# A two-layer stretch of a decoder: sparse self-attention whose keys and values are copied by DMA instead of projected once per offset

## The chip, the core and the metric

The kernel runs on one NeuronCore of a Trainium2 chip. Five engines have their own instruction streams and meet at semaphores: TensorE (PE in the profile; PEld is its weight load), VectorE (DVE), ScalarE (ACT), GpSimd (POOL) and SyncE (SP, which here only issues DMAs). Every stream is executed in the order in which it was written down; an instruction that waits holds up all that stand behind it on its engine. The metric is the device time of one execution in microseconds, lower is better.

## What is computed

A pre-norm decoder of four layers on x of shape (8, 256, 128), float32, each layer with a self-attention, a cross-attention and a feed-forward part. Each part reads the layer norm of x and adds its result to x:

```python
x = x + _L1_ffn_ref(_layernorm(x), W_r, W_k, W_v, mu_r, mu_k)
x = x + _L2_attn_ref(_layernorm(x), W_qkv, b_qkv, W_proj, b_proj)
x = x + _L2_xattn_ref(_layernorm(x), ctx, Wq, bq, Wk, bk, Wv, bv, Wo, bo)
```

The change lies in `L2_attn`: 16 heads of 8 channels, 256 tokens per batch, and a mask under which token i sees only the tokens i - o for o in 0, 1, 2, 4, 8, 16, 32, 64, 128, where they exist. So each token has at most nine keys; the softmax is over nine scores per head. The kernel computes it without a score matrix: for each offset o it needs the keys and values of token i - o beside the query of token i. `L2_xattn`, which follows, is a dense cross-attention of 256 queries on 512 keys per batch, 16 heads.

## The kernel before

**Layout.** x stays in SBUF with tokens on the partitions, two half batches of 128 tokens for each of the 8 batches. `E.xt(b, back)` is the transposed norm of batch b (channels on partitions, tokens along the free dimension), with 128 zero columns ahead of it, so that `back=o` reads the tokens moved down by o.

**`_l2_attn` (L1066).** It works on half batches t = 2b + half. `weigh(t)` projects the query (`fa_qps`, L1084), and then, for each offset, projects keys and values of the moved tokens (`fa_kvps`, L1097): 8 projections for the first half and 9 for the second, each of 256 output columns. VectorE multiplies each key block by the query into `fa_pr` (L1098), ScalarE copies the values to `fa_v` (L1101). Then come the sum over the 8 channels of a head (L1107), the key bias (L1108), the mask, the softmax over the offsets (L1113 to L1118, exp on ScalarE L1115), values times weights on GpSimd (L1120), and the first step of the sum over the offsets, also on GpSimd (L1122). `apply(t)` ends the sum (L1128 to L1132), transposes (`fa_tps`), applies the output projection (`fa_yps`), adds to x, and after the second half takes the norm for the next layer. `through` runs `weigh(t)` and then `apply(t - 1)`, so one half batch's GpSimd work lies beside the next one's projections. Both use two buffers per tile.

**Two places.** Batches 0 and 1 are run by `_middle` (L1215) beside the end of the layers before. The other six batches, and the last three of the four `_l1_ffn` units that come ahead of them, are a *guest*: a Python generator (`rest`, L1220) which `_heads_attention` advances while it writes down the instructions of `L2_xattn`. Each `yield` is a place where the host's own instructions come in between.

**The host.** `_heads_attention` (L463) writes down 128 steps t, 16 heads for each of 8 batches. Step t has the scores for the row maxima (`mh_sps`, two 128x512 tiles, three PSUM banks in all; VectorE reduces each to `mh_nm`, L527), the transposed scores of the step eight earlier with their exponentials (`mh_bsps`, L581), and now and then a product with the values (`mh_ops`). `visit(rate)` (L663) advances the guest by `rate` yields a step: 1.25 here (L697). Ahead of head 9 of batch b, the guest is advanced until batch b + 1 has been normed (L686). Matrix products and transposes of the host and of the guest go through `mm` and `turn_over` (L447), which keep them in the order in which the program wrote them. The other engines' instructions are ordered by a scheduler with its own estimates.

**DMAs.** For each batch, keys and queries of `L2_xattn` are spread over partitions by 12 SBUF to SBUF DMAs on SP's queue (`mh_k`, L422, and `mh_q`, L427). Ahead of the first scores, ScalarE fills those buffers with constants (L368), in memory that is free only when the layers before are done.

Of the kernel before, what the change touches and what calls it, by code (L numbers as in the profile page):

```python
# [40 lines left out]
P = 128  # L41
# [418 lines left out]
            f()  # L460


def _heads_attention(E, ctx, causal=False, mask=None, key_bias=None, gate=False, guest=None, known=(0,)):  # L463

# [190 lines left out]
    def normed(b, z):  # L657
        _normed(E, b, z, pg, turn_over)

    normed_already = set(range(B) if guest is None else known)  # L660
    credit = [0.0]

    def visit(rate):  # L663

        credit[0] += rate
        while credit[0] >= 1:
            credit[0] -= 1
            normed_already.add(next(guest, None))
# [4 lines left out]
    while t < end or todo:  # L673
        now[0] = t
        b, h = divmod(t, H)
        if b + 1 < B:
            if h == 0:
                early, spread, values = hd.steps(b + 1)
            if causal:

                at = {2: early[:1], 3: early[1:2], 4: early[2:], 13: [values]}
                at.update({5 + i: spread[i : i + 1] for i in range(6)})
            else:
                at = {6: early[:1], 8: spread[:1], 9: spread[1:2] + early[1:], 13: spread[5:] + [values]}
                at.update({10 + i: spread[2 + i : 3 + i] for i in range(3)})
            while h == 9 and b + 1 not in normed_already:  # L686
                visit(1)
            for f in at.get(h, ()):
                f()
        if gate and b < B and h == 6:  # L690
            gate_of(b)
        if t < H * B:
            maxima(t)
            if t % 4 == 3:
                turn(t // 4)
        if guest:
            visit(1.25 if 1 in known else 2.4 if t < 9 else 1.4)  # L697
        if t % 4 == 1 and 4 < t < H * B + 2:
            turned(t // 4 - 1)
        if 0 <= t - lag < H * B:  # L700
            exps(t - lag)
        c = t - lag - 4
        if c % 4 == 0 and 0 <= c < H * B:
            combine(c // 4)
        for f in todo.pop(t, ()):
            f()
        if t == H * (B - 2) + 12 + free:
            E.draining()
        t += 1


def _l0(E, names, given_up):

    nc = E.nc
    with ExitStack() as scope, ExitStack() as first:
# [38 lines left out]
                pass  # L754
        for _ in queries:
            pass
        _heads_attention(E, scope, mask=(m, mt), guest=steps)


def _l2_xattn(E, ctx):  # L760
    guest, E.guest = E.guest, None
    _heads_attention(E, ctx, guest=guest, known=(0, 1))


def _l3_attn(E, ctx):
# [254 lines left out]
def _l1_ffn(E, ctx, side="left"):  # L1020
# [6 lines left out]
    def unit(g):  # L1027
        mixed = []
        for i, n in enumerate(("mu_r", "mu_k")):
            t = wk.tile([P, 2, S], F32, name="rk_t")  # L1030
            nc.vector.tensor_scalar(t, E.xt2(g, 1), rest[:, i : i + 1], None, ALU.mult)
            m = wk.tile([P, 2, S], F32, name=f"rk_m{i}")
            nc.vector.scalar_tensor_tensor(m, E.xt2(g), W(n), t, ALU.mult, ALU.add)
            mixed.append(m.rearrange("p b t -> p (b t)"))
        yield
        mr, mk = mixed
        ps = E.banks.rk.tile([P, 512], F32, tag="g", name="rk_kps")
        E.mm(ps, W("wk"), mk, start=True, stop=True)
        k = wk.tile([P, 512], F32, name="rk_k")
        nc.scalar.activation(k, ps, AF.Relu)  # L1040
        nc.scalar.activation(k, k, AF.Square)
        yield
        ps = E.banks.rk.tile([P, 4, D], F32, tag="g", name="rk_rps")
        for t in range(4):
            E.mm(ps[:, t, :], mr[:, t * P : t * P + P], W("wr"), start=True, stop=True)
        r = wk.tile([P, 4, D], F32, name="rk_r")
        nc.scalar.activation(r, ps, AF.Sigmoid)
        yield
        ps = E.banks.rk.tile([P, 4, D], F32, tag="g", name="rk_ops")
# [16 lines left out]
def _l2_attn(E, ctx):  # L1066


    nc, W = E.nc, E.w("L2_attn")
    wk = ctx.enter_context(E.tc.tile_pool(name="fa", bufs=2))  # L1070
    scale = DH ** -0.5
    NO = len(OFFS)
    heads = lambda a: a.rearrange("p (h d) -> p h d", d=DH)
    st = {}

    def weigh(t):
        b, half = divmod(t, 2)
        at = slice(half * P, half * P + P)
        if half == 0:
            E.pre_add(b, W("bo"))  # L1080
        offs = [o for o in OFFS if o < P * (half + 1)]
        no = len(offs)
        ps = E.banks.fa.tile([P, D], F32, tag="g", name="fa_qps")
        E.mm(ps, E.xt(b)[:, at], W("wqkv")[:, :D], start=True, stop=True)  # L1084
        q = wk.tile([P, D], F32, name="fa_q")
        nc.vector.tensor_tensor(q, ps, W("b")[:, :D], ALU.add)

        yield
        qb = wk.tile([P, D], F32, tag="fa_s", name="fa_qb")
        nc.gpsimd.tensor_tensor(qb, q, W("b")[:, D : 2 * D], ALU.mult)  # L1090
        pr = wk.tile([P, NO, D], F32, name="fa_pr")
        v = wk.tile([P, NO, D], F32, name="fa_v")
        for i in range(0, no, 2):
            n = min(2, no - i)
            ps = E.banks.fa.tile([P, 2, 2 * D], F32, tag="g", name="fa_kvps")
            for j in range(n):
                E.mm(ps[:, j, :], E.xt(b, offs[i + j])[:, at], W("wqkv")[:, D:], start=True, stop=True)  # L1097
            nc.vector.tensor_tensor(  # L1098
                pr[:, i : i + n, :], ps[:, :n, :D], q.unsqueeze(1).to_broadcast([P, n, D]), ALU.mult
            )  # L1100
            nc.scalar.copy(v[:, i : i + n, :], ps[:, :n, D:])  # L1101
            yield
        sb = wk.tile([P, H], F32, name="fa_sb")
        nc.vector.tensor_reduce(sb, heads(qb), AX.X, ALU.add)
        sc = wk.tile([P, NO, H], F32, name="fa_sc")
        a = sc[:, :no, :]
        nc.vector.tensor_reduce(a, pr[:, :no, :].rearrange("p o (h d) -> p o h d", d=DH), AX.X, ALU.add)  # L1107
        nc.vector.tensor_tensor(a, a, sb.unsqueeze(1).to_broadcast([P, no, H]), ALU.add)  # L1108
        if half == 0:
            nc.vector.tensor_tensor(a, a, W("fenwick")[:, :no].unsqueeze(2).to_broadcast([P, no, H]), ALU.add)  # L1110
        red = wk.tile([P, H], F32, name="fa_red")
        wide = red.unsqueeze(1).to_broadcast([P, no, H])
        nc.vector.tensor_reduce(red, a.rearrange("p o h -> p h o"), AX.X, ALU.max)  # L1113
        nc.vector.tensor_tensor(a, a, wide, ALU.subtract)
        nc.scalar.activation(a, a, AF.Exp, scale=scale)  # L1115
        nc.vector.tensor_reduce(red, a.rearrange("p o h -> p h o"), AX.X, ALU.add)
        nc.vector.reciprocal(red, red)
        nc.vector.tensor_tensor(a, a, wide, ALU.mult)  # L1118
        v4 = v[:, :no, :].rearrange("p o (h d) -> p o h d", d=DH)
        nc.gpsimd.tensor_tensor(v4, v4, a.unsqueeze(3).to_broadcast([P, no, H, DH]), ALU.mult)  # L1120

        nc.gpsimd.tensor_tensor(v[:, :4, :], v[:, :4, :], v[:, 4:8, :], ALU.add)  # L1122
        st[t] = v, no

    def apply(t):
        v, no = st.pop(t)
        o = wk.tile([P, D], F32, tag="fa_s", name="fa_o")
        nc.vector.tensor_tensor(v[:, :2, :], v[:, :2, :], v[:, 2:4, :], ALU.add)  # L1128
        nc.vector.tensor_tensor(o, v[:, 0, :], W("b")[:, 2 * D :], ALU.add)
        nc.vector.tensor_tensor(o, o, v[:, 1, :], ALU.add)  # L1130
        if no > 8:
            nc.vector.tensor_tensor(o, o, v[:, 8, :], ALU.add)  # L1132
        ps = E.banks.fa.tile([P, P], F32, tag="g", name="fa_tps")
        E.turn_over(ps, o)
        ot = wk.tile([P, P], F32, name="fa_ot")
        nc.scalar.copy(ot, ps)
        yield
        ps = E.banks.fa.tile([P, D], F32, tag="g", name="fa_yps")
        E.mm(ps, ot, W("wo"), start=True, stop=True)
        nc.vector.tensor_tensor(E.x[:, t, :], ps, E.x[:, t, :], ALU.add)  # L1140
        if t % 2:
            z = _norm(E, t // 2)
            yield
            yield
            yield
            _normed(E, t // 2, z, E.banks.ln, E.turn_over)
            yield t // 2

    def through(g, n, ahead=lambda g: ()):

        first, end = 4 * g, 4 * (g + n)
        for t in range(first, end + 1):
            if t < end:
                if t % 4 == 0:
                    yield from ahead(t // 4)
                yield from weigh(t)
            if t > first:
                yield from apply(t - 1)

    return through  # L1160


def _middle(E, names, then):
# [8 lines left out]
    if names != MIDDLE:  # L1172
        for n in names:
            with ExitStack() as scope:
# [4 lines left out]
                    "L2_attn": _l2_attn,  # L1179
                }[n](E, scope, *([pg] if n in MIDDLE[:3] else []))  # L1180
                if n == "L2_attn":
                    _run(unit(0, 4))
                    continue
                for g in range(4):
                    _run(unit(g) or ())
# [26 lines left out]
    begun = E.beginning(then)  # L1212
    if guest:
        next(begun)
    _run(fa(0, 1))  # L1215
    if guest:
        next(begun, None)
    psum.close()
# [1 line left out]
    def rest():  # L1220
# [4 lines left out]
        with ExitStack() as own:  # L1225
            if not guest:
                g = banks(own, "mid_pg2", 6)
                E.banks = SimpleNamespace(fa=g, rk=g, ln=g)
            yield from fa(1, 3, _l1_ffn(E, own))
        last.close()  # L1230
        E.close_weights()

# [434 lines left out]
```

## Time and profile before

| | us |
|---|---|
| runs | 1818.8, 1821.27, 1822.99 (median 1821.27) |
| profiled execution | 1820.01 |
| its span, first to last instruction | 1818.2 |
| `fa` instructions of `_l2_attn`, first and last start | 782.2 to about 1211 |
| first scores of `L2_xattn` | 912.8 |
| last row maxima of `L2_xattn` | 1278.0 |
| TensorE busy over the span | 1483.6 (82%) |
| VectorE busy | 1147.1 (63%) |
| ScalarE busy | 874.4 (48%) |
| GpSimd busy | 515.3 (28%) |

The profile gives, for each stretch of time, how long each engine had an instruction in execution, how many instructions there were, the clock that TensorE was granted (1.00 is full speed), the mean busy share of the 16 DMA engines and the bytes that they moved. For each tile it gives the instructions that write or read it, with the shortest, median and longest duration in ns. For each idle stretch it names the instruction that ended it. "SPq" is the issue of a DMA by SP.

### The profile page before, as it was taken

How to read it: one execution, taken by the hardware profiler on the slowest of the kernel's cores; microseconds unless marked ns; L12 is line 12 of the kernel's file. 1: busy time of each engine (PE TensorE's matmuls, PEld its weight loads, DVE VectorE, ACT ScalarE, POOL GpSimd, SP SyncE). 2: the span in 40 equal slices, each digit the busy share in tenths (PEclk: the TensorE clock that was granted, in tenths of full speed). 3: DMA queues.
4: the chain of work that ended last, by engine and by line, in shares of the span. 5: the costliest groups of instructions: out<-in, count | busy, mean ns of one | idle time of the engine just before them, and what ended most of it. 6: DMA issues, size and time to landing. Idle time of an engine off the chain costs nothing. (4 is left out here: it accounts for less than half of the span.)

```text
span 1818.2 us, 29293 instructions
## 1 busy us (share of the span) xinstructions
PE 1483.6 (82%) x10099; PEld 1070.8 (59%) x10137; DVE 1147.1 (63%) x3869; ACT 874.4 (48%) x1791; POOL 515.3 (28%) x1002
## 2 busy tenths in 40 slices
PE   5689999999989989787378888879635999799976
PEld 3456677766655556455256665656314777677753
DVE  3567666675636676777377777767584665455546
ACT  7245455555642445222645556557412566466621
POOL 3122222222101121333323433331225333344321
PEclk8799999999999999887689999989755999899977
DMA  4011101114000000000111111011002221111000
GB/s 150 12 36 35 26 14 37 35 32 154 12 1 1 1 1 1 0 1 1 26 43 35 36 32 32 14 36 37 17 23 82 66 54 49 47 51 49 26 1 23
DMA packets 47235, 60.42 MB, mean 33 GB/s; under 512 B 5232, under 2 KB 36976, under 8 KB 46448
## 3 DMA queue, kind: packets, MB, share of 16 engines
q1 hardware_dynamic: 44720, 56.99, 11.8%
q8 instruction: 80, 1.31, 0.3%
q10 hardware_dynamic: 2368, 1.57, 0.3%
q14 instruction: 67, 0.55, 0.1%
HBM read 14.50 MB, written 1.05 MB: 9 GB/s over the span
## 5 line engine op out<-in xcount | busy, mean ns | idle before, releaser
L448 PE MATMUL mh_sps<-mh_k,mh_q 96*128 96x512 f32 (+2 forms) x1024 | 321.7, 396 | 46.7 <-DMA mh_q<-mh_qp 16.1
L448 PE MATMUL mh_bsps<-mh_q,mh_k 128*128 128x256 f32 (+1 forms) x1536 | 351.0, 334 | 6.9 <-ACT mh_e L581 4.1
L581 ACT ACTIVATE mh_e<-mh_bsps 128x512 f32<-128x512 f32 x512 | 280.8, 599 | 114.3 <-PE mh_bsps L448 107.1
L448 PEld LDWEIGHTS mh_bsps<-mh_q,mh_k 128*128 128x128 f32 x1536 | 264.6, 197 | 31.8 <-issue 6.7
L448 PEld LDWEIGHTS mh_sps<-mh_k,mh_q 96*128 96x128 f32 x1024 | 171.7, 201 | 94.5 <-issue 37.4
L508 DVE CUSTOM_DVE_ANT_0 mh_rest<-mh_sps,mask_b 128x512 bf16<-128x512 f32 x256 | 167.2, 685 | 84.5 <-PE mh_sps L448 81.3
L448 PE MATMUL mh_ops<-mh_e,mh_v 128*32 128x256 f32 (+1 forms) x3072 | 201.7, 372 | 11.1 <-ACT mh_e L568 10.6
L527 DVE TENSOR_REDUCE mh_nm<-mh_sps 128x1 f32<-128x512 f32 x256 | 164.8, 681 | 32.9 <-PE mh_sps L448 32.5
L448 PEld LDWEIGHTS mh_ops<-mh_e,mh_v 128*32 128x32 f32 x3072 | 96.5, 111 | 81.4 <-ACT mh_e L568 22.1
L568 ACT ACTIVATE mh_e<-mh_bsps 128x384 f32<-128x384 f32 x256 | 116.5, 494 | 49.4 <-PE mh_bsps L448 29.6
L197 POOL TENSOR_SCALAR ln_rstd<-ln_mv 128x2 f32<-128x2 f32 x96 | 22.7, 237 | 392.9 <-DVE ln_mv L195 392.9
L508 DVE CUSTOM_DVE_ANT_0 mh_rest<-mh_sps,km_q 128x128 bf16<-128x128 f32 (+1 forms) x256 | 80.0, 350 | 66.1 <-PE mh_sps L448 63.6
L508 DVE CUSTOM_DVE_ANT_0 mh_rest<-mh_sps,causal 128x128 bf16<-128x128 f32 (+1 forms) x256 | 79.6, 353 | 63.4 <-PE mh_sps L448 46.3
L534 POOL CAST mh_hi<-mh_nm 128x8 fp32r<-128x8 f32 x128 | 25.1, 196 | 332.4 <-DVE mh_nm L508 203.8
L215 ACT COPY xt<-ln_ps 128x256 f32<-128x256 f32 x96 | 36.0, 375 | 160.7 <-PE ln_ps L214 81.6
L546 ACT CAST mh_m<-mh_mps 8x256 fp32r<-8x256 f32 x128 | 46.3, 362 | 97.6 <-PE mh_mps L451 95.7
L611 ACT COPY mh_osb<-mh_ops 128x256 f32<-128x256 f32 x128 | 47.7, 372 | 85.8 <-PE mh_ops L448 85.5
L869 ACT ACTIVATE moe_si<-moe_gps 128x512 f32<-128x512 f32 x64 | 38.0, 597 | 102.1 <-PE moe_gps L867 81.4
L448 PE MATMUL mh_bsps<-mask_t,ident 128*128 128x512 bf16 x219 | 85.0, 388 | 0.4 <-ACT mh_e L581 0.4
L867 PE MATMUL moe_ups<-xt,w_L_ffn 128*128 128x512 f32 x128 | 68.9, 621 | 7.0 <-ACT moe_si L869 4.8
L878 PEld LDWEIGHTS moe_dps<-w_L_ffn,moe_act 128*128 128x128 f32 x512 | 64.6, 200 | 15.9 <-issue 7.5
L201 DVE TENSOR_SCALAR ln_z<-x,ln_mv,ln_rstd 128x128 f32<-128x128 f32 x128 | 42.7, 374 | 48.5 <-POOL ln_rstd L198 48.4
(357 smaller groups left out, 3118.6 us busy)
## 6 DMA issues: line engine op xcount, KB each, us to landing
mh_k<-mh_kp SPq DMA_DIRECT2D x64, 256.0 KB
mh_q<-mh_qp SPq DMA_DIRECT2D x256, 64.0 KB
mh_k<-mh_kp SPq DMA_DIRECT2D x64, 128.0 KB
w_L_ffn<-in_w_L_ffn SPq DMA_DIRECT2D x2, 1558.0 KB
w_L_attn<-in_w_L_attn SPq DMA_DIRECT2D x2, 1056.0 KB
ctx_t<-in_ctx_t SPq DMA_DIRECT2D x4, 512.0 KB
mh_q<-mh_m ACTq DMA_DIRECT2D x128, 8.0 KB
w_L_ffn<-in_w_L_ffn SPq DMA_DIRECT2D x2, 687.0 KB
```

The costliest lines, as they stand in the source:

```text
L201: (engine or nc.vector).tensor_scalar(z[:, q, :], E.x[:, 2 * b + q, :], mv[:, q, 0:1], rstd[:, q : q + 1], ALU.subtract, ALU.mult)
L215: E.nc.scalar.copy(E.xt(b), ps.rearrange("p q t -> p (q t)"))
L448: return self.E.tc.keep_in_program_order(self.E.nc.tensor.matmul(*a, **kw))
L508: nc.vector.tensor_tensor_reduce(rest[:, : scores.shape[1]], scores, lowered, -1.0, -FLOOR, ALU.add, ALU.min, accum_out=at)
L527: nc.vector.tensor_reduce(u.nm[:, c, col], ps, AX.X, ALU.max, negate=True)
L546: nc.scalar.copy(m, ps[:8].rearrange("p c q -> p (c q)"))
L568: nc.scalar.activation(e, ps, AF.Exp, scale=scale)
L581: nc.scalar.activation(e, ps, AF.Exp, scale=scale)
L611: nc.scalar.copy(osbs[b][:, u4 % 2, :], ops)
L867: nc.tensor.matmul(ps, W("w13")[:, o : o + P], xt, start=True, stop=True)
L869: nc.scalar.activation(si, pgate, AF.Silu)
L878: nc.tensor.matmul(ps[:, t, :], act[:, c, t * P : t * P + P], W("w2")[:, o : o + P], start=c == 0, stop=c == 1)
```

## The change

Keys and values of a batch are projected once, without an offset, with the query in the same matrix product (384 columns, `fa_ps`). VectorE adds the bias and writes them to slot 0 of one tile `fa_kv` of [128, 2 halves, 9 offsets, 256], of which there is a single buffer. For the other offsets, 15 DMAs on SP's queue copy slot 0 down by o partitions: rows o to 127 of both halves from rows 0 to 127 - o, and the first o rows of the second half from the last o rows of the first. For the lowest offset the first of these has 127 partitions, then 126, 124, 120, 112, 96 and 64. The rows of the first half that no token reaches are zeroed once, on ScalarE. Products of key and query, and of value and weight, are written over `fa_kv`, and both halves of a batch go through one softmax. `one_batch(b)` has 13 yields and is not overlapped with the next batch; the generator's loop runs over batches.

`_middle` runs only batch 0 instead of batches 0 and 1; batch 1 becomes the guest's first work. The pace of the guest in `L2_xattn` becomes 1.6 yields a step for the first nine steps and 1.2 after. In `_l1_ffn` two tiles share the buffers of two others. What `L0_xattn` does is the same, written with a function for its pace.

```diff
...
-def _heads_attention(E, ctx, causal=False, mask=None, key_bias=None, gate=False, guest=None, known=(0,)):
+def _heads_attention(E, ctx, causal=False, mask=None, key_bias=None, gate=False, guest=None, pace=None):
...
-    normed_already = set(range(B) if guest is None else known)
+    normed_already = set(range(B) if guest is None else (0,))
...
-            visit(1.25 if 1 in known else 2.4 if t < 9 else 1.4)
+            visit(pace(t))
...
-        _heads_attention(E, scope, mask=(m, mt), guest=steps)
+        _heads_attention(E, scope, mask=(m, mt), guest=steps, pace=lambda t: 2.4 if t < 9 else 1.4)
 def _l2_xattn(E, ctx):
     guest, E.guest = E.guest, None
-    _heads_attention(E, ctx, guest=guest, known=(0, 1))
+    _heads_attention(E, ctx, guest=guest, pace=lambda t: 1.6 if t < 9 else 1.2)
...
-            m = wk.tile([P, 2, S], F32, name=f"rk_m{i}")
+            m = wk.tile([P, 2, S], F32, tag=f"rk_m{i}", name=f"rk_m{i}")
-        k = wk.tile([P, 512], F32, name="rk_k")
+        k = wk.tile([P, 512], F32, tag="rk_m1", name="rk_k")
-        r = wk.tile([P, 4, D], F32, name="rk_r")
+        r = wk.tile([P, 4, D], F32, tag="rk_m0", name="rk_r")
...
     nc, W = E.nc, E.w("L2_attn")
+    one = ctx.enter_context(E.tc.tile_pool(name="fa1", bufs=1))
     wk = ctx.enter_context(E.tc.tile_pool(name="fa", bufs=2))
     scale = DH ** -0.5
     NO = len(OFFS)
...
+    kv = one.tile([P, 2, NO, 2 * D], F32, name="fa_kv")
+
+    nc.scalar.copy(
+        kv[:, 0, 1:, :].rearrange("p o c -> p (o c)"), E.plain[:, 0:1].to_broadcast([P, (NO - 1) * 2 * D])
+    )
+    heads = lambda a: a.rearrange("p s o (h d) -> p (s o) h d", d=DH)
+
+    def one_batch(b):
+        E.pre_add(b, W("bo"))
+        q = wk.tile([P, 2, D], F32, name="fa_q")
+        for s in range(2):
+            ps = E.banks.fa.tile([P, 3 * D], F32, tag="g", name="fa_ps")
+            E.mm(ps, E.xt(b)[:, s * P : s * P + P], W("wqkv"), start=True, stop=True)
+            nc.vector.tensor_tensor(kv[:, s, 0, :], ps[:, D:], W("b")[:, D:], ALU.add)
+            nc.vector.tensor_tensor(q[:, s, :], ps[:, :D], W("b")[:, :D], ALU.add)
+        yield
+        for i, o in enumerate(OFFS):
+            if 0 < o < P:
+                nc.sync.dma_start(kv[o:, :, i, :], kv[: P - o, :, 0, :])
+                nc.sync.dma_start(kv[:o, 1, i, :], kv[P - o :, 0, 0, :])
+            elif o:
+                nc.sync.dma_start(kv[:, 1, i, :], kv[:, 0, 0, :])
+        yield
+        yield
+        k, v = kv[:, :, :, :D], kv[:, :, :, D:]
+        nc.vector.tensor_tensor(k, k, q.unsqueeze(2).to_broadcast([P, 2, NO, D]), ALU.mult)
+        yield
+        sc = wk.tile([P, 2, NO, H], F32, name="fa_sc")
+        nc.vector.tensor_reduce(sc.rearrange("p s o h -> p (s o) h"), heads(k), AX.X, ALU.add)
+        nc.vector.tensor_tensor(
+            sc[:, 0, :, :], sc[:, 0, :, :], W("fenwick").unsqueeze(2).to_broadcast([P, NO, H]), ALU.add
+        )
+        red = wk.tile([P, 2, H], F32, name="fa_red")
+        wide = red.unsqueeze(2).to_broadcast([P, 2, NO, H])
+        by_head = sc.rearrange("p s o h -> p s h o")
+        nc.vector.tensor_reduce(red, by_head, AX.X, ALU.max)
+        nc.vector.tensor_tensor(sc, sc, wide, ALU.subtract)
+        nc.scalar.activation(sc, sc, AF.Exp, scale=scale)
+        yield
+        nc.vector.tensor_reduce(red, by_head, AX.X, ALU.add)
         nc.vector.reciprocal(red, red)
...
+        nc.vector.tensor_tensor(sc, sc, wide, ALU.mult)
+        for s in range(2):
+            v4 = v[:, s, :, :].rearrange("p o (h d) -> p o h d", d=DH)
+            nc.gpsimd.tensor_tensor(v4, v4, sc[:, s, :, :].unsqueeze(3).to_broadcast([P, NO, H, DH]), ALU.mult)
+
+        for s in range(2):
+            nc.gpsimd.tensor_tensor(v[:, s, :4, :], v[:, s, :4, :], v[:, s, 4:8, :], ALU.add)
+        yield
+        yield
+        o = wk.tile([P, 2, D], F32, name="fa_o")
+        nc.vector.tensor_tensor(v[:, :, :2, :], v[:, :, :2, :], v[:, :, 2:4, :], ALU.add)
+        nc.vector.tensor_tensor(o, v[:, :, 0, :], v[:, :, 1, :], ALU.add)
+        nc.vector.tensor_tensor(o, o, v[:, :, 8, :], ALU.add)
+        yield
+        ps = E.banks.fa.tile([P, 2, P], F32, tag="g", name="fa_tps")
+        for s in range(2):
+            E.turn_over(ps[:, s, :], o[:, s, :])
+        ot = wk.tile([P, 2, P], F32, name="fa_ot")
         nc.scalar.copy(ot, ps)
         yield
...
+        ps = E.banks.fa.tile([P, 2, D], F32, tag="g", name="fa_yps")
+        for s in range(2):
+            E.mm(ps[:, s, :], ot[:, s, :], W("wo"), start=True, stop=True)
+        E.add(b, ps)
+        z = _norm(E, b)
+        yield
+        yield
+        yield
+        _normed(E, b, z, E.banks.ln, E.turn_over)
+        yield b
+
+    def through(first, end, ahead=lambda g: ()):
+
+        for b in range(first, end):
+            if b % 2 == 0:
+                yield from ahead(b // 2)
+            yield from one_batch(b)
     return through
...
-                    _run(unit(0, 4))
+                    _run(unit(0, 8))
...
-    _run(fa(0, 1))
+    _run(fa(0, 1 if guest else 2))
...
-            yield from fa(1, 3, _l1_ffn(E, own))
+            yield from fa(1 if guest else 2, B, _l1_ffn(E, own))
```

More of the change, by code (lines that the diff above doesn't have):

```diff
@@ L1072, in _l2_attn @@
     NO = len(OFFS)
[L1073 to L1086, printed above, removed]
-        yield
[L1089 to L1116, printed above, removed]
-        nc.vector.reciprocal(red, red)
[L1118 to L1135, printed above, removed]
+    kv = one.tile([P, 2, NO, 2 * D], F32, name="fa_kv")
@@ L1136, in apply @@
         nc.scalar.copy(ot, ps)
         yield
[L1138 to L1158, printed above, removed]
+        ps = E.banks.fa.tile([P, 2, D], F32, tag="g", name="fa_yps")
```

## The prediction

> **What bounds the kernel now.** I read the windows of busy time first, split at the two places where `_l2_attn` runs: 782 to 912 us (beside the layers before), 912 to 1211 (guest in `L2_xattn`), and 1220 to 1280 (the host alone). Columns: busy us and count for PE, PEld, DVE, ACT, POOL, then granted clock, DMA share, GB/s.
>
> ```profile
> 782.00:863.00 81.00, 61.10 (x234) 42.44 (x235) 61.32 (x162) 23.30 (x56) 28.75 (x29) 0.75 0.00 1
> 863.00:912.00 49.00, 17.11 (x58) 11.25 (x56) 17.63 (x51) 28.65 (x27) 14.58 (x18) 0.67 0.13 30
> 912.00:1211.00 299.00, 248.08 (x1739) 180.69 (x1740) 219.62 (x547) 155.87 (x345) 106.06 (x180) 0.93 0.14 34
> 1220.00:1280.00 60.00, 56.85 (x486) 40.42 (x480) 43.65 (x88) 42.90 (x89) 12.33 (x36) 1.00 0.12 29
> ```
>
> The host alone is bound by PE (57 of 60 us). Between 863 and 912 nothing is full: that is a chain of waits. The same windows for the row maxima (L527, DVE) count steps, two to a step:
>
> ```profile
> 912.00:1211.00 299.00, 121.69 (x188) 0.93 0.14 34
> 1220.00:1280.00 60.00, 39.73 (x64) 1.00 0.12 29
> ```
>
> So the host alone takes 60/32 = 1.88 us a step, and with the guest 299/94 = 3.18. Of the 299 us, 94 x 1.88 = 176 are the host's, and about 72 of the 248 busy us are the guest's. By the rows of the tiles, and 8 projections starting in 1.89 us on the timeline:
>
> ```profile
> L448 PE MATMUL fa_kvps<-w_L_attn,xt x204: 377/379/634, 932.0 to 1192.7; 128*128 128x256 f32 x102
> PE fa_tps L451 <- DVE fa_o L1132: 8.8, 1, 8.8
> ```
>
> 204 x 0.24 = 48 us are key and value projections. The rest of the 299, 51 us, is PE idle; lines of the waits that name `fa` tiles (such as the second above) make 21 of it. The guest's own chain hardly stalls PE today: a half batch's work has the next one's projections beside it.
>
> How the stage begins, and what the operations of the chain take (timeline, then tiles; ns are shortest, median, longest):
>
> ```profile
> 862.99 3.60 ACT L368 CAST mh_k<-plain 64x4096 fp32r<-64x4096 f32 x1 [2.35 <-DVE x L1014]
> 912.80 2.35 PE L448 MATMUL mh_sps<-mh_k,mh_q 96*128 96x512 f32 x4 [7.57 <-DMA mh_q<-mh_qp]
> L1107 DVE TENSOR_REDUCE fa_sc<-fa_pr x16: 1161/1278/1353, 822.9 to 1194.0; 128x128 f32<-128x1024 f32 x8, 128x144 f32<-128x1152 f32 x8
> L1120 POOL TENSOR_TENSOR fa_v<-fa_v,fa_sc x16: 1965/2092/2196, 843.4 to 1199.0; 128x1024 f32<-128x1024 f32 x8, 128x1152 f32<-128x1152 f32 x8
> L1122 POOL TENSOR_TENSOR fa_v<-fa_v x16: 1261/1272/1287, 845.5 to 1201.3; 128x512 f32<-128x512 f32 x16
> L427 SPq DMA_DIRECT2D mh_q<-mh_qp x8: 613/613/649, 906.2 to 911.0; - x8
> ```
>
> SP needs 0.613 us for each DMA, and the last of these was usable 912.8 - 911.0 = 1.8 us after its issue began.
>
> **Part 1, the start of the stage: a gain.** Only batch 0 stands ahead of `L2_xattn`. In the changed order ScalarE does, from the first fill on, three fills (3.6 each), one of 0.76, the key bias 0.68, the value copy 0.58, the norm's copy 0.37, another fill 3.6 and the query bias 0.47: 17.3 us. Before, query bias to first scores took 912.8 - 905.7 = 7.1. If the fills start at 863 as now, scores begin at 887. PE loses some 50 projections (12 us) between 782 and 863, where it is busy 61 of 81 us; I take 3 us of it, bounds 0 and 8 (the layers before have their own chains). Start 884, 28.5 us earlier. Batch 0's DMAs are issued near 784 and needed after some 35 us of older VectorE work: free. The zero fill (2048 columns, half a 4096 fill: 1.8 us of ACT, once) lies where ACT is busy 23 of 81 us: free; uncovered, 1.8. Shared tags in `_l1_ffn`: each tile's last reader precedes the new writer anyway; free (1 us a group at worst).
>
> **Part 2, PE, ACT and DVE work of the guest: a gain.** Projections become 7 batches x 2 halves x 2 passes of 384 columns; eight such passes (L918) took 2.75 us, so 0.344 x 28 = 9.6. Transposes and output 6, norms and the three `_l1_ffn` units 15: 31 in place of 72. DVE falls by some 3 us a batch (nine products of 0.41 become one of about 2.6; one softmax for two), ACT by nine copies of 0.37. These two are not the bound here and get nothing. Idle of other causes stays: 51 - 21 = 30, of which I keep 25 as the start is smoother. Stage: 176 + 31 + 25 = 232 us, 67 less than 299. Parts 1 and 2 together: 95 us to the good, before any new wait.
>
> **Part 3, the chain of one batch: a loss.** The batches no longer overlap each other, and PE's order is fixed: between `fa_ps` and `fa_tps` the changed order has the scores of 7, 6, 7, 7, 7 and 6 steps (5 for batch 1), mean 6.6 x 1.88 = 12.4 us of PE work. Then PE stands until the chain is through, with all host steps behind it. VectorE's order is worse: from the key product (L1099) to the last sum (L1127) stands one row maximum at most, so it waits for ScalarE and GpSimd with the maxima behind it. From the end of the DMAs the chain is: product and reduction over 2304 elements, 2.6 each (twice L1107's 1.3); mask, max, subtract, exp, sum, reciprocal, multiply about 3.1; GpSimd 2 x 2.19 + 2 x 1.27 = 6.9; three sums 1.6; handovers 0.3: 17.1. Projection and bias ahead: 2. With D from first issue to last landing, PE's stall is S = 2 + D + 17.1 - 12.4 = D + 6.7; for batch 1, where five steps of scores alone take 6.5 us, D + 12.6. Sum over 7 batches: 7D + 53.
>
> **D, which no row shows.** A batch has 15 DMAs, 1.8 MB in rows of 1 KB. Low end: issue sets the pace, 15 x 0.613 + 1.8 = 11. That needs all 16 engines. The rows here that move much use outer dimensions of 8, 16 or 128. The Trainium skill, page "DMA: Bandwidth & Descriptors", section "Why a DMA increments its semaphore by 16 and not by 1", says that a copy goes to the largest number of engines up to 16 that divides its slowest dimension, starting with the lowest, and gives 127 partitions as the case of one engine. No copy before has such a shape, so the trace neither confirms nor denies it. By that rule 127, 126, 124 and 120 partitions use 1, 14, 4 and 15 engines, and engine 0 gets 254 + 18 + 62 + 16 + 34 (the larger others) + 8 + 11 (small ones) = 403 rows. Time per row:
>
> ```profile
> 904.00:914.00 10.00, 2.43 (x7) 1.34 (x6) 0.39 (x1) 0.85 (x2) 1.78 (x3) 0.50 0.20 52
> 10.00:20.00 10.00, 3.59 (x4) 1.34 (x5) 2.58 (x4) 9.94 (x7) 2.32 (x4) 1.00 0.87 339
> ```
>
> The first window holds 512 rows of 1 KB (`mh_q`) in 0.20 x 160 = 32 engine us: 62 ns. The second, long loads, 339/(16 x 0.87) = 24.4 GB/s an engine: 42 ns. I take 50, since one long queue lies between the two: 403 x 0.05 + 0.6 + 1.8 = 22.6 us. With 42 ns 19.3, with 62 ns 27.6. By the issue row alone the loss is 7 x 11 + 53 = 130; by the page's rule 7 x 22.6 + 53 = 211. I take the rule[...]; its other end stays in the range. `mh_k` and `mh_q` spreads now stand behind these DMAs on SP and on engine 0; they would land some 6 us after D, inside the 17 us chain that PE waits for, so they add nothing; were the chain short, they would be late next. A stalled PE also restarts slowly (clock 0.50 in the window 904 to 914): 0 to 2 us a batch, in the range only, because VectorE sets the pace of the first steps.
>
> **Sum.** -95 + 211 = +116 on the profiled 1820.0: 1936. That execution is 1.3 us under the median of 1821.3, so no correction is made. A difference of 0.2% (3.6 us) is about what the measurement can tell.
>
> **Rivals.**
> A (forecast, 0.72): few engines carry the copies; 1913 at 42 ns, 1936, 1971 at 62 ns (1985 with a slow restart).
> B (0.17): the copies do spread over 16 engines; -95 + 130 = +35: 1855. For it: the 12 spreads per batch of today use 8 or 16 engines. Against: the divisibility of 127.
> C (0.08), faster: the chain is hidden, so that only the PE relief is left. The place is PE's wait at `fa_tps`; the price is S, and it decides at 95/7 = 13.6 us. With row maxima slipping in and steps slower than 1.88 us (the present 3.18 x 6.6 = 21 us would cover all but S = 8 with D = 11), 7 x 8 = 56: 1781. Against: the written order of VectorE, and that steps get slow only by stalling.
> Same (0.03): B with S near 13.6.
>
> **How the numbers follow.** 1936 is A at 50 ns. The range 1850 to 1990 takes in B and A with its slow restart and leaves out C, and A with still slower rows. Faster 0.08, same 0.03, slower 0.89.
>
> **What would show it.** Scores of `L2_xattn` beginning near 884 (part 1). Some 31 us of guest work on PE up to the last `fa_yps` (part 2). PE waits naming `fa_tps` of 25 to 35 us for each of seven batches, and VectorE's key product waiting for DMA `fa_kv` 10 us or more; one DMA engine far busier than the mean share. Waits of about 18 us at `fa_tps` and none of VectorE on DMA would be B. Wrong altogether: no wait at `fa_tps`, or an end of the guest earlier than 1211 us.

## The result, and the profile after

The changed kernel takes 1954.01 us (median of four runs, 1953.41 to 1954.51), against 1822.13 for the kernel before, run beside it: ratio 1.0727, interval 1.0708 to 1.0745. The profiled execution has a span of 1951.6 us, 133.4 more than before, where the prediction had 116 more.

The windows, with the same columns as before: the layers before; the fills ahead of `L2_xattn`; guest and host together; most of the host alone.

```profile
782.00:863.00 81.00, 45.52 (x192) 27.63 (x192) 58.16 (x140) 22.12 (x46) 29.31 (x27) 0.81 0.08 23
863.00:887.00 24.00, 4.54 (x19) 2.47 (x19) 1.63 (x6) 23.86 (x12) 5.49 (x10) 0.66 0.27 66
887.00:1325.00 438.00, 212.53 (x1434) 145.95 (x1438) 220.03 (x437) 135.98 (x271) 108.03 (x172) 0.71 0.19 50
1325.00:1400.00 75.00, 70.89 (x608) 50.05 (x604) 53.08 (x114) 51.91 (x106) 14.26 (x42) 0.96 0.16 37
```

The guest's stage has grown from 299 to 438 us although PE has less to do in it (213 us busy for 248). PE stands idle for 225 us of the stage, and its granted clock is 0.71 in place of 0.93. No other engine is full either: VectorE is busy for half the time. A stage in which everybody is half idle is a chain of waits. Two of the lines of waits (waiting engine and line, releaser, us in all, times, longest) show its links, VectorE for the copies and PE for VectorE's last sum:

```profile
PE fa_tps L451 <- DVE fa_o L1127: 154.4, 7, 32.9
DVE fa_kv L1099 <- DMA fa_kv<-fa_kv: 77.6, 7, 14.7
```

The first guest batch in the timeline (start, us, engine, instruction; in brackets the idle time before it and what ended it):

```profile
886.95 1.19 PE L448 MATMUL mh_sps<-mh_k,mh_q 96*128 96x512 f32 x2 [9.76 <-DMA mh_q<-mh_qp]
...
889.91 1.95 SPq L1093 DMA_DIRECT2D fa_kv<-fa_kv  x3
...
891.96 11.52 SPq L1092 DMA_DIRECT2D fa_kv<-fa_kv  x4
...
909.89 0.60 SPq L1095 DMA_DIRECT2D fa_kv<-fa_kv  x1
...
912.00 2.56 DVE L1099 TENSOR_TENSOR fa_kv<-fa_kv,fa_q 128x2304 f32<-128x2304 f32 x1 [14.67 <-DMA fa_kv<-fa_kv]
...
920.75 4.33 POOL L1118 TENSOR_TENSOR fa_kv<-fa_kv,fa_sc 128x1152 f32<-128x1152 f32 x2 [25.14 <-DVE fa_sc L1115]
...
927.55 0.69 DVE L1125 TENSOR_TENSOR fa_kv<-fa_kv 128x512 f32<-128x512 f32 x1 [6.88 <-POOL fa_kv L1121]
...
929.31 0.66 PE L451 MATMUL fa_tps<-ident,fa_o 128*128 128x128 f32 x2 [32.92 <-DVE fa_o L1127]
```

Read it downwards: scores begin at 886.95, the copies are issued from 889.91 on, the key product starts 22.1 us after the first issue (this is D), the chain behind it takes 17.3 us, and PE has by then waited 32.9 us at the transpose. The four issues in the second SP line took 11.52 us, where four of 0.65 would be 2.6: SP was held for some 9 us. What the DMA engines did meanwhile (window 889 to 914 in 40 slices of 0.625 us; the first line is the mean busy share of the 16 engines in tenths, the second what they moved):

```profile
DMA  0000000000000000001744324676768464450000
GB/s 0 0 0 2 3 7 0 11 13 13 18 25 23 25 25 25 23 25 41 213 157 95 48 80 84 151 195 177 220 210 261 154 159 120 128 203 21 0 0 0
```

For some 5 us the whole core moves 25 GB/s, and then up to 261. The prediction took 24.4 GB/s for one engine at long loads, so this plateau reads as one engine at work, and fifteen that wait for SP to issue; the runs with one more copy test it.

### The profile page after: what moved, and what is told of

Read it like the earlier page. It is cut to its first block, busy times and chain, and to the rows that moved or that the text cites. A ratio compares the mean times of both kernels' runs of the same rounds, so it can differ in the third digit from the quotient of the medians.

```text
span 1951.6 us, 28659 instructions
## 1 busy us (share of the span) xinstructions
PE 1441.3 (74%) x9865; PEld 1025.5 (53%) x9865; DVE 1139.9 (58%) x3701; ACT 854.6 (44%) x1704; POOL 507.4 (26%) x986
## 5 line engine op out<-in xcount | busy, mean ns | idle before, releaser
L448 PE MATMUL mh_sps<-mh_k,mh_q 96*128 96x512 f32 (+2 forms) x1024 | 325.9, 401 | 71.0 <-DMA mh_q<-mh_qp 20.7
L581 ACT ACTIVATE mh_e<-mh_bsps 128x512 f32<-128x512 f32 x512 | 276.6, 599 | 123.5 <-PE mh_bsps L448 96.0
L448 PEld LDWEIGHTS mh_bsps<-mh_q,mh_k 128*128 128x128 f32 x1536 | 268.6, 200 | 55.1 <-ACT mh_e L581 20.5
L448 PE MATMUL mh_ops<-mh_e,mh_v 128*32 128x256 f32 (+1 forms) x3072 | 209.7, 385 | 11.0 <-ACT mh_e L568 10.9
L448 PEld LDWEIGHTS mh_ops<-mh_e,mh_v 128*32 128x32 f32 x3072 | 99.1, 114 | 86.4 <-ACT mh_e L568 22.1
L451 PE MATMUL fa_tps<-ident,fa_o 128*128 128x128 f32 x14 | 4.8, 444 | 154.4 <-DVE fa_o L1127 154.4
L534 POOL CAST mh_hi<-mh_nm 128x8 fp32r<-128x8 f32 x128 | 24.7, 193 | 356.8 <-DVE mh_nm L508 204.6
L448 PE MATMUL mh_bsps<-mask_t,ident 128*128 128x512 bf16 x256 | 99.3, 388 | 0.4 <-ACT mh_e L581 0.4
```

Of the source, the lines that this page charges most:

```text
L448: return self.E.tc.keep_in_program_order(self.E.nc.tensor.matmul(*a, **kw))
L534: nc.gpsimd.tensor_copy(hi, nm)
L581: nc.scalar.activation(e, ps, AF.Exp, scale=scale)
```

## The experiments

### Cutting the odd copies

```diff
-                nc.sync.dma_start(kv[o:, :, i, :], kv[: P - o, :, 0, :])
+                m = (P - o) // 16 * 16
+                nc.sync.dma_start(kv[o : o + m, :, i, :], kv[:m, :, 0, :])
+                if o + m < P:
+                    nc.sync.dma_start(kv[o + m :, :, i, :], kv[m : P - o, :, 0, :])
```

> Each copy of o to 127 is cut in two: the largest multiple of 16 partitions first (112, 112, 112, 112, 112, 96, 64), and the remaining 15, 14, 12 and 8 in a copy of their own: 19 DMAs a batch in place of 15, the same bytes. Theory A (few engines carry the copies): first issue to key product falls from 22 to 26 us to about 14 (19 x 0.613 + 1.8), the key product's waits on DMA from 77.6 us to 20 at most, and the time by 7 x 10 = 70 us to about 1884. Rival, SP's issue sets D: four more issues make each batch 2.5 us longer, about 1970. Rival, the chain behind the copies is all of the loss: within 10 us of 1954.

Measured: 1909.06 us, ratio to before 1.0473 (1.045 to 1.0497): 45 us back, not 70. D (first issue to key product) fell in the seven batches from 22.1, 22.2, 25.7, 25.6, 23.0, 23.1, 23.7 (mean 23.6) to 15.6, 15.9, 23.2, 23.2, 15.8, 15.4, 15.6 (mean 17.8). So the direction of the forecast holds, and its size does not: 19 issues at 0.65 us and 2.1 to the landing make 14.5, and five of the seven batches are within 1.5 us of that. The other two kept a D above 23. SP's own waits name why:

```profile
SPq L1095 <- DMA mh_q<-mh_m: 13.4, 2, 6.8
```

Twice a copy waits some 7 us for a small DMA of the host's, issued by ScalarE. The changed kernel has the same wait in the same two batches (9.6 us in the two together). The copies share no data with that DMA, but they share a semaphore (the counter that tells when a DMA is done): by the trace the DMAs of the stage take eight of them in turn, 24 to 26 DMAs each in the changed kernel, and each of these waits is for the DMA that used the copy's own semaphore last.

### No copies

```diff
-        for i, o in enumerate(OFFS):
-            if 0 < o < P:
-                nc.sync.dma_start(kv[o:, :, i, :], kv[: P - o, :, 0, :])
-                nc.sync.dma_start(kv[:o, 1, i, :], kv[P - o :, 0, 0, :])
-            elif o:
-                nc.sync.dma_start(kv[:, 1, i, :], kv[:, 0, 0, :])
```

> The copies by offset are left out (slots 1 to 8 of both halves are zeroed once and hold what the kernel leaves there), so that only slot 0 is right; every other instruction stays. Theory A says that D was about 23 of a stall of about 30 us, but that the rest of the chain (17 us behind 13 row maxima) is not hidden either: S = 17 for six batches, 13 for the first, stage 232 + 115 = 347 us in place of 434, about 1867. Rival, the copies are all of the loss: about 1727, no PE wait at fa_tps. Rival, the copies cost nothing: 1954.

Measured: 1825.28 us, ratio 1.0013 (1.0002 to 1.0023), 42 us below the forecast and near neither rival. Leaving the copies out takes 129 us away. But without them nothing is gained over before either, so the rest of the new order eats the whole gain of parts 1 and 2. The stage, which begins at 878.7 here, and PE's waits, of this kernel:

```profile
879.00:1200.00 321.00, 208.66 (x1434) 144.26 (x1437) 217.64 (x435) 135.76 (x270) 110.75 (x172) 0.80 0.12 27
```

```profile
PE fa_tps L451 <- DVE fa_o L1122: 62.6, 6, 12.3
PE mh_sps L448 <- DVE mh_nm L527: 28.9, 14, 15.4
```

PE idles 112 us of this stage, 63 of it at the transposes and 29 for row maxima that stand behind the guest's chain in VectorE's order.

The omission takes away more than the copies of the stage. Batch 0's copies are gone too, and its transpose comes at 847.0 us instead of 855.4, so 8 of the 129 us lie ahead of the stage. And VectorE's instructions come out in another order: in five of the seven batches 12 to 14 row maxima stand inside the chain, which then takes 23.2 to 24.7 us, where the changed kernel has four at most. So the 129 us are the copies with that order, which no run separates.

### The early start by itself, in the kernel before

```diff
-            visit(1.25 if 1 in known else 2.4 if t < 9 else 1.4)
+            visit((2.0 if t < 9 else 1.3) if early else 2.4 if t < 9 else 1.4)
...
-    _run(fa(0, 1))
+    _run(fa(0, 1 if guest else 2))
```

(`fa` counts groups of two half batches here in the old line and batches in the new one; `through` runs `2 * g` to `2 * n`.)

> The kernel before, with one part of the change: only batch 0 runs ahead of the cross-attention, batch 1 is the guest's first work, pace 2.0 yields a step for nine steps and 1.3 after. Projections per offset stay. Part 1 of the prediction gives 26 us at the start; batch 1 costs the guest 16 us of PE and about 5 of waits: about 1816. Rival, the early start gains nothing because batch 1 has no cover in the first nine steps (15 us more of waits): 1825 to 1830. Rival, the start is worth the full 26: 1795.

Measured: 1827.59 us, ratio 1.0029 (1.0017 to 1.0041): the rival held, not the 1816 forecast. Row maxima start 23 us earlier (890.2 instead of 913.6) and end 9 us later (1286.9 instead of 1278.0). The batch that no longer delays the start comes back as guest work in a stage where PE is busy for four fifths of the time. An early start, with the pace that goes with it, is worth nothing here.

### One more copy of 127 partitions, and one of 112

```diff
+    spare = one.tile([P, 2, 2 * D], F32, name="fa_spare")
...
+        nc.sync.dma_start(spare[:127, :, :], kv[:127, :, 0, :])
         for i, o in enumerate(OFFS):
```

> Ahead of the copies of each batch stands one more, of 127 partitions to a spare tile that nobody reads (254 rows of 1 KB). Theory A, with 127 partitions on one engine: D grows by 254 rows at 45 to 50 ns, 11 to 13 us, 7 batches 80 to 89 us: about 2038. Rival, the copies spread over 16 engines and the issue sets D: 0.6 to 1 us a batch, about 1960.

> The changed kernel with one more copy ahead of each batch's copies, of 112 partitions instead of the 127 of the run before, into the same spare tile (its data are not used). Theory A (one engine carries a copy of 127 partitions): 16 engines take these 224 rows, so a batch pays one issue on SP, 0.6 us, and at most 0.6 us of transfer: 1958 to 1963 us, key products waiting some 1 us longer a batch. If it is the bytes and not the number of engines, this copy costs nearly what 127 partitions cost (8.4 us a batch): 2005 to 2013.

Measured: 2013.02 us (ratio 1.1045, 1.1021 to 1.1069) with 127 partitions; 1955.92 us (ratio 1.0738, 1.0712 to 1.0763) with 112. An extra 254 rows cost 59 us in the first case, 8.4 a batch, less than the forecast of 2038; an extra 224 rows cost 2 us in the second, which its interval does not tell from nothing. SP's issues in the first guest batch, 127 above and 112 below:

```profile
891.43 0.74 SPq L1091 DMA_DIRECT2D fa_spare<-fa_kv  x1
...
892.23 21.69 SPq L1094 DMA_DIRECT2D fa_kv<-fa_kv  x4
```

```profile
892.92 0.70 SPq L1091 DMA_DIRECT2D fa_spare<-fa_kv  x1
...
893.68 11.82 SPq L1094 DMA_DIRECT2D fa_kv<-fa_kv  x4
```

The same four issues take 11.5 us in the changed kernel, 11.8 with 112 more partitions and 21.7 with 127 more: 10.2 us for 254 rows of 1 KB, 40 ns each, one engine's 25 GB/s. In the run with two such copies the plateau is twice as long (window 889 to 924, slices of 0.875 us):

```profile
GB/s 0 1 2 5 7 12 14 25 23 25 25 23 25 25 23 25 25 23 25 23 25 25 23 25 25 158 179 74 64 171 217 217 179 237 143 46 171 75 0 0
```

The number of partitions decides here, not the bytes. This agrees with the rule of the Trainium skill that the prediction rested on ("DMA: Bandwidth & Descriptors", "Why a DMA increments its semaphore by 16 and not by 1"), for these two counts.

### Cutting only the copy of 127

```diff
-                nc.sync.dma_start(kv[o:, :, i, :], kv[: P - o, :, 0, :])
+                m = 112 if o == 1 else P - o
+                nc.sync.dma_start(kv[o : o + m, :, i, :], kv[:m, :, 0, :])
+                if o == 1:
+                    nc.sync.dma_start(kv[o + m :, :, i, :], kv[m : P - o, :, 0, :])
```

> The changed kernel with only the copy of 127 partitions cut in two (112 and 15); the 126, 124 and 120 stay whole. Theory A, sharpened by the traces (one engine moves the 127 rows alone at 25 GB/s, SP is held in an issue behind it, and only then are the other DMAs issued at 0.65 us each): 16 issues make 10.4 us and 2.1 us to the landing, so D near 13 (20 in the two batches that also wait for another DMA), three issues fewer than in the run that cut all four: 1890 to 1900 us. Rival: the 124 (by the rule 4 engines) and 126 hold the queue as well, so that the cut of all four was needed: D 16 to 18, 1910 to 1925.

Measured: 1907.09 us (ratio 1.0473, 1.0437 to 1.0508), the same as with all four cut, and between the forecast (1890 to 1900) and its rival (1910 to 1925). D has a mean of 17.8 in both. The 127 is the whole of what cutting brings; three issues fewer did not help, because a single issue behind the uncut 124 is still held:

```profile
896.42 1.99 SPq L1093 DMA_DIRECT2D fa_kv<-fa_kv  x1
```

### The issues on two queues

```diff
                 if o + m < P:
-                    nc.sync.dma_start(kv[o + m :, :, i, :], kv[m : P - o, :, 0, :])
-                nc.sync.dma_start(kv[:o, 1, i, :], kv[P - o :, 0, 0, :])
+                    nc.scalar.dma_start(kv[o + m :, :, i, :], kv[m : P - o, :, 0, :])
+                nc.scalar.dma_start(kv[:o, 1, i, :], kv[P - o :, 0, 0, :])
```

> All four odd copies cut as in the first run, and the 19 DMAs of a batch shared: eight of them from SP, eleven small ones from ScalarE's queue. Theory (with no long queue on one engine, the issues pace the copies: 19 x 0.65 + 2.1 = 14.5 against measured 15.6): now 11 x 0.65 + 2.1 = 9.3, so some 6 us a batch less: 1865 us, and down to 1855 if SP's waits for another DMA in two batches go as well. Rival 1: the 16 engines' own pace sets D (1.84 MB): D stays at 15 and the time at 1905 to 1912. Rival 2: ScalarE, which now spends 7 us a batch on issues ahead of exponentials, gives it back: 1900 or more.

Measured: 1906.32 us (ratio 1.0463, 1.0439 to 1.0487), against 1.0473 with one queue: a miss, and no gain that can be told from nothing. D did fall where nothing else interfered (10.4, 10.8, 12.4 and 12.0 in batches 1, 5, 6 and 7), so the issues did pace the copies. In batches 2 to 4 it was 20.4, 25.0 and 23.7. Two of SP's lines show the queues waiting for each other: copies for a DMA of the host's, and the host's spreads for copies.

```profile
SPq L422 <- DMA fa_kv<-fa_kv: 24.6, 3, 13.7
...
SPq L1093 <- DMA mh_q<-mh_m: 14.4, 2, 7.7
```

In batches 5 to 7, where D was 3 to 5 us shorter than on one queue, the chain behind it took 20.6 to 23.2 us instead of 17.2, with 7 to 10 row maxima in it instead of none: what D gave, the chain took back. PE waited less at `fa_tps` (101 us instead of 152) and more for ScalarE's exponentials, one queue above and two below:

```profile
PE mh_bsps L448 <- ACT mh_e L581: 4.3, 3, 2.2
```

```profile
PE mh_bsps L448 <- ACT mh_e L581: 35.0, 9, 7.8
```

This is the price that the rival of 1900 or more had named: ScalarE, with copies to issue, is late with what PE needs. How much of the rest the cross waits of batches 2 to 4 make, no run separates.

### Another order

```diff
-        for b in range(first, end):
-            if b % 2 == 0:
-                yield from ahead(b // 2)
-            yield from one_batch(b)
+        for b in range(1, end):
+            more = b + 1 < end
+            yield from chain(b, ahead((b + 1) // 2) if more and b % 2 else plain())
+            if more:
+                yield from project(b + 1)
+            yield from tail(b)
...
```

`project` is the projection and the (cut) copies, `chain` goes from the key product to the sums, `tail` is the transpose, the output projection and the norm, and `plain` is seven bare yields. Batch 1 is projected ahead of the stage; the pace is 1.8 and 1.15. So several things change at once, and what each is worth no run separates.

> The changed kernel in another order: copies cut as in the first run, the next batch's projection and copies are issued right behind this batch's sums, and the feed-forward units run beside the chain, so that PE has 13 to 14 steps between a batch's projection and its transpose. Theory (what is left without copies, 1825, is the chain in PE's and VectorE's order): D and the chain are covered for PE (13.5 x 1.88 = 25 us against 15.6 before and 19 us of the rest); VectorE still stands behind GpSimd in its order, up to 7 us a batch: 1727 + 0 to 49, forecast 1775. Rival: the remainder is not the chain but a slow clock and restarts of PE, or the guest's own work: 1825 or more.

Measured: 1810.15 us, ratio 0.9938 (0.9917 to 0.9959), 35 us above the 1775 forecast. The wait that made the loss is gone: where the changed kernel had 154.4 us at `fa_tps` in seven waits, this one has 6.0 in one. Waits of PE, and then of VectorE:

```profile
PE mh_sps L448 <- DVE mh_nm L527: 49.2, 24, 10.4
...
PE fa_tps L451 <- DVE fa_o L1133: 6.0, 1, 6.0
```

```profile
DVE fa_kv L1131 <- POOL fa_kv L1127: 29.3, 6, 7.3
```

D is 15.3 to 16.6, as in the quiet batches of the cut version, and the chain is even longer, 19.4 to 30.2 us. So it was not the chain's length that cost the time, but that too little stood beside it. The first and the last line show where the time stands now: PE for row maxima of VectorE, and VectorE behind GpSimd. The next version moves VectorE's last sums over the offsets to GpSimd:

```diff
-        nc.vector.tensor_tensor(v[:, :, :2, :], v[:, :, :2, :], v[:, :, 2:4, :], ALU.add)
-        nc.vector.tensor_tensor(o, v[:, :, 0, :], v[:, :, 1, :], ALU.add)
-        nc.vector.tensor_tensor(o, o, v[:, :, 8, :], ALU.add)
+        nc.gpsimd.tensor_tensor(v[:, :, :2, :], v[:, :, :2, :], v[:, :, 2:4, :], ALU.add)
+        nc.gpsimd.tensor_tensor(o, v[:, :, 0, :], v[:, :, 1, :], ALU.add)
+        nc.gpsimd.tensor_tensor(o, o, v[:, :, 8, :], ALU.add)
```

> The reordered kernel of the run before (1810 us), with its last three sums over offsets on GpSimd, behind its own products and sums, instead of on VectorE. Theory (what is left above the floor is VectorE standing in its order behind GpSimd, 29 us of waits for it in that trace, and PE 49 us for the row maxima queued behind them): GpSimd takes 2 to 3 us more a batch in the shadow of other work, and 20 to 30 us of the waits go: 1780 to 1790 us. Rival: those waits were hidden, or GpSimd's norms queued behind the longer GpSimd chain take their place: 1805 to 1815.

Measured: 1804.14 us, ratio 0.9917 (0.989 to 0.9944): by the ratios 4 us less than with the sums on VectorE, but the intervals overlap, so it is not told from nothing, and it is not the 20 to 30 forecast. PE's waits for the maxima fell only from 49.2 to 35.9 us, and its wait at `fa_tps`, now for GpSimd, rose from 6.0 to 10.1. The rival (1805 to 1815) was nearer.

Then the pace alone:

```diff
-pace=lambda t: 1.8 if t < 9 else 1.15
+pace=lambda t: 1.6 if t < 9 else 1.0
```

> The same, with the guest spread wider: 1.6 and 1.0 guest units a step instead of 1.8 and 1.15. In the reordered run the guest ended 70 us before the last row maxima of the host, so there is room for some 10 % more steps in the guest's time. Theory (each batch still waits for its own chain somewhere): 5 to 15 us less than its neighbour in this job. Rival (the chain is covered already at the faster pace): the same within 3 us, or slower if the guest is still running when the host ends.

Measured: 1788.62 us, ratio 0.9823 (0.9796 to 0.985), 15.5 us under the run before it, by the pace alone. This version is 1.8% below the kernel before, and its interval is clear of 1. Whether the kernel before would gain from another pace too was not tried.

```profile
PE mh_sps L448 <- DVE mh_nm L527: 25.0, 12, 3.6
```

The guest ends no later than at the faster pace (last `fa_yps` near 1191 in both), and 204 row maxima come before that end where 188 did, so the eight added host steps lie in time that PE had idled.

```diff
-pace=lambda t: 1.6 if t < 9 else 1.0
+pace=lambda t: 1.4 if t < 9 else 0.87
```

> The reordered kernel with the sums on GpSimd, the guest spread wider still: 1.4 and 0.87 guest units a step (1788.6 us at 1.6 and 1.0; 1804.1 at 1.8 and 1.15). In the trace at 1.6 and 1.0 the guest ended where it did at the faster pace, near 1191, and the host 54 us later, so some of each chain is still waited for. Theory: 5 to 12 us less again, 1777 to 1784. Rival: the cover is complete, and only the guest's end moves back: within 3 us of 1788, or above it if the guest outlasts the host.

Measured: 1791.3 us, ratio 0.9848 (0.9829 to 0.9868): no further gain. The rival held.

And the reordered kernel of 1810 us (sums on VectorE, pace 1.8 and 1.15) without its copies:

```diff
         yield
-        for i, o in enumerate(OFFS):
-            if 0 < o < P:
...
     def chain(b, beside):
```

> The reordered kernel of 1810 us without its copies: the slots of the other offsets are zeroed once and keep what each batch's products leave in them, so its output is not the reference's. Theory (with 26 us of PE work between a projection and its transpose the copies lie off the path): 1803 to 1812 us, against 129 us for the same omission in the changed kernel. Rival (the copies still cost by traffic in the DMA engines and on SP ahead of the host's own transfers): 1780 or less.

Measured: 1791.45 us, ratio 0.9841 (0.9815 to 0.9866). That is 19 us by the medians, 18 by the ratios, against 129 for the same omission in the changed kernel. Some 8 to 9 of it are the stage's start (row maxima from 891.3 instead of 899.9), and they are there already at batch 0's transpose (848.1 instead of 856.9), as in the changed kernel. So the copies are mostly, not wholly, off the path. The result lies between the forecast (1803 to 1812) and its rival (1780 or less).

## Why the prediction was right, and where its sum was not

**The mechanism held, point by point.** One engine carries the 127-partition copy (plateau at 25 GB/s, 8.4 us a batch for one more of it, no clear cost for 112). The chain behind the copies was put at 17.1 us and took 17.2 to 17.7 where no row maximum or one came between, and 18.6 to 19.1 in the three batches where three or four did. VectorE's key product was to wait 10 us or more for the copies, and waited 8.7 to 14.7. PE's stall was put at 25 to 35 us a batch. At `fa_tps` alone three batches show less, but there part of the same stall stands at an earlier instruction, as in the fourth guest batch, where the two make 28.6; so all seven lie between 26.0 and 32.9:

```profile
1119.65 1.19 PE L448 MATMUL mh_sps<-mh_k,mh_q 96*128 96x512 f32 x2 [16.35 <-issue]
...
1133.13 0.69 PE L451 MATMUL fa_tps<-ident,fa_o 128*128 128x128 f32 x2 [12.29 <-DVE fa_o L1127]
```

**Part 1** had the start at 884; it is 886.95, the value it gave if the layers before do not end earlier. Batch 0's DMAs were called free there: without any copies scores begin at 878.7, 8 us earlier, and VectorE does batch 0's key product at 785.7 instead of 821.1. So a term put at nothing, batch 0's copies with the order that VectorE has beside them, took the relief of 3 us and more.

**Part 2** put projections, transposes and outputs at 9.6 + 6 us of PE; they took 23.8 (11.9, 4.8 and 7.2). A projection pass was counted at 0.344 us and made 0.42 here. Most of the rest is the transposes and outputs, which come directly behind the stall. The same 14 transposes in the changed kernel and in the reordered one at pace 1.6 and 1.0, where no long wait stands ahead of them (ns are shortest, median, longest):

```profile
L451 PE MATMUL fa_tps<-ident,fa_o x14: 421/433/476, 929.3 to 1317.8; 128*128 128x128 f32 x14
```

```profile
L451 PE MATMUL fa_tps<-ident,fa_o x14: 271/273/299, 921.0 to 1187.7; 128*128 128x128 f32 x14
```

There the two groups take 2.7 and 4.4 us, not 4.8 and 7.2. "0 to 2 us a batch, in the range only" for the slow restart belonged in the sum: this guest work alone shows 1.2 us a batch, and the whole of PE some 2 (213 us busy, where 89 steps at 1.88 and the 31 of the guest make 198; an estimate by the prediction's own price of a step). The stage has 88 or 89 steps beside the guest, where 94 had been counted from the old order; the others, 9 us or more, moved behind it. That is the written order and not the speed: 176 row maxima begin before the last `fa_yps` in the changed kernel, and as many without copies and with cut ones.

**Part 3, D.** The forecast of 22.6 us against a measured mean of 23.6 is close, but it was a sum of other terms. It took engine 0 as one queue of 403 rows, beside which the other issues ran. In fact SP is held in an issue while the first 254 rows drain (some 9 us), and only then are the remaining DMAs issued at 0.65 us each: the two follow each other. At 40 ns a row the prediction's own form would have given 403 x 0.04 + 2.4 = 18.5. The 50 ns that it chose hid the missing term. That the total came out near was luck in this term. In two batches D also has the wait for the host's DMA, which no step foresaw.

**The sum.** In the prediction's form, with D at nothing, the change gives 53 - 95 = -42 us, and the copies add 7 x 22.6 = 158. The run without copies separates the two: +4 and 129. Both terms were wrong, by +46 and by -29, and the total is off by 17. The first: without copies the stage took 321 us, where 232 + 53 = 285 had been counted. PE idled 112 us in it, not 25 + 53 = 78, and was busy 209 us with 88 steps, not 207 with 94. The 29 us of waits for row maxima behind the chain in VectorE's order were named in the text and not priced. The second: PE's idle time in the stage fell by 113 us (225 to 112) when the copies went, 16 a batch, though D was 23.6, and 8 more lie ahead of the stage. So a microsecond of D was not a microsecond of loss: without copies the chain itself was longer, by the row maxima that VectorE then does inside it. Of the 133 us between the two profiles, 6 lie behind the last row maxima (span less last maxima: 540.2 before, 546.3 after), and nothing here explains them.

**"The spreads add nothing"** held: PE's waits for them are 13.0 us in the changed kernel, 9.8 of that at the stage's start.

**The rivals.** B, copies over 16 engines, would have been 1855; the run with cut copies shows that this state costs 1909, so its price was too low too: D is 17.8 in that run, not 11, and the first term misses there as well. C, a covered chain, is not what the change does, but the reordered version comes near it. At 1789 us it has some 32 us of the 95 that parts 1 and 2 had counted.

## What to carry to other kernels

A copy of nearly the same bytes cost 8.4 us a batch with 127 partitions and 0.3 with 112: for SBUF copies like these, cut such counts into a multiple of 16 and the rest, and look for a stretch in which the whole core moves one engine's rate. A cheaper operation placed as a serial chain costs what stands behind it in each engine's order: count the work that lies between producer and consumer on every engine, VectorE's too, before you count the saving. Price a term by taking it away, and look what else went with it: two wrong terms gave a total near the measured one here, by luck.

## What the runs showed that was not expected

- SP is held inside an issue while one engine drains a long share: four issues took 11.5 us with one copy of 127 partitions under way, and 21.7 with two. The others that stand behind on SP, and 15 idle engines, wait with it.
- Copies waited 5 to 8 us for a DMA of another queue with which they share no data, in the changed kernel and in the versions with cut copies on one or two queues: the DMAs take eight semaphores in turn, and the copy's own had been used by that DMA last.
- Sharing the issues between two queues brought D down to 10.4 us in a quiet batch and nothing in the total.
- A slower pace of the guest ended the whole earlier by 15.5 us, and a still slower one brought nothing more.
